# A third buffer for W1 and W2, products of zeros at the lowest rank, a wider port rule in the planner, and new ranks

## The chip, the core and the metric

The kernel runs on one core of one Trainium2 chip. The metric is the device time of one execution in microseconds (us); less is better. The engines are TensorE (PE in the profile, with its weight loads as PEld), VectorE (DVE), ScalarE (ACT), GpSimd (POOL) and SyncE (SP), which issues nearly all transfers.

## What is computed

x has the shape (4, 2048, 256) in float32. An attention block, here a long convolution with a gate, and a grouped linear block follow one another, each behind a layer norm and with the input added again:

```python
uv = silu(layernorm(x) @ uv_w)
u, v = split(uv, 2, axis=-1)
# _tno: convolution of v along the sequence with a kernel that a small network gives
a = concatenate([t_zero, t_pos, zeros, t_neg])           # t_* = _rpe(position) * GAMMA ** |position|
y = irfft(rfft(a, n=2 * n) * rfft(v, n=2 * n))[:, :n]
x = x + (u * y) @ o_w
# grouped block: 8 groups of 1024 tokens, no activation between its two products
h1 = einsum('gmh,goh->gmo', layernorm(x) in groups, W1) + b1
h2 = einsum('gmo,gho->gmh', h1, W2) + b2
x = x + h2
```

`_rpe` is a network on the position: three layers of layer norm, silu and a 32x32 product, and an output layer of the same kind.

## The kernel before

The program has two parts. First, Python functions record operations, one list for all engines (`Recorder`, line 69, with the recorders V, G, A, T and S for DVE, POOL, ACT, PE and SP). Then `issue_order` (line 287) sorts the whole list, and one loop issues it. So nearly all instructions have the line L1123 in the profile; they are told apart by the names of their tiles.

The stages, in the words that the profile uses for their tiles:

- `rpe_network` (line 621) computes the kernel of the convolution at 4096 positions. Each of its four layers makes two products ph, ACT writes their squares sq and a copy d, PE sums the squares into pvar (products with 4 columns), DVE makes a reciprocal root by three Newton steps on 128x32 tiles (nve, nh, ny, nt) and spreads it to ne, PE transposes ne into pr, DVE multiplies d by pr, and ACT makes z, from which the next layer's ph comes. All constants of the network are in one transfer, par; the first ph needs w0, which DVE makes from par. `rpe_transform` (line 705) makes the spectrum am from the result.
- `stage_a` (line 570) loads a quarter of a batch (xa), normalizes it (st_a, mv_a, ve_a, rs_a, nb_a, xn_a), transposes it (pt_a, xnt), makes v through the product pv, and POOL adds and subtracts halves of v into c.
- `prepare` splits c into residues of the polynomial ring for one batch b and half h (ra and others). `stage_b` (line 883) does for each of eight residues r a product pf with a matrix from `mats`, two multiplications with am on DVE (y, far), a product acc back, and then combinations on DVE; its `end` makes four tiles tk with which POOL multiplies the gate gt. `gate` (line 873) makes gt from the product pu.
- `stage_d` (line 1025) makes the product po of gt and o_w, adds it to x, normalizes, and multiplies with the folded weights wt (product pff) into the output.
- `stage_w` (line 811) folds the two weight matrices of a group g into one: the product pw over eight pieces of the inner dimension, loaded in four pairs of transfers w1 and w2 (256 KB each, offsets 0, 2, 4 and 6). ACT adds a bias to each w1 in place. pw lies in the pool ps_w, which has a single buffer; the products of zeros (`warm`) write to a tile of the same buffer, so that a pw comes only after the last of them. DVE makes wt from pw at the end.

```python
w1s = io.tile([P, oc, D], F32, tag="w1", bufs=WB, name=f"w1_{g}_{o}")
S.dma_start(w1s, w1[g].rearrange("(p a) h -> p a h", a=na)[:, o : o + oc, :])
```

The profile calls both tiles w, without group and offset. Each of the two tags has WB buffers; with 2, piece 4 of a group waits until the products of piece 0 have read their buffers.

What sets the order: each operation has a rank, 20 times its batch plus a value from the table `PLACE` (line 156). `place` (line 273) looks up the most exact key, so "w.6.l.1" (group 6, loading, second pair) goes ahead of "w.6"; keys with "first" and "last" hold for batches 0 and 3 alone. `issue_order` then steps through a modelled run: of all operations whose inputs and buffers are there, it takes the one that can start earliest, and of those that can start at the same time the one of lowest rank. Its durations come from `Operation.cost` (line 116). Three details of this model are touched:

- `port`: an operation of DVE with two inputs of at least 64 columns in SBUF, and any operation of POOL with inputs, occupy one shared port in the model, one after the other.
- `COLD`, `IDLE`: after an idle of more than IDLE ns, PE's operations cost twice as much for COLD ns.
- A tile takes a buffer of its tag in the order of the lowest ranks of its operations.

Twelve products of zeros (`WARM_UP`) are recorded with the ranks "warm.0" to "warm.11", the lowest numbers of all or nearly so: they stand at the head of PE's queue, ahead of the first ph.

Of the kernel before, what the change touches and what calls it, by code (L numbers as in the profile page):

```python
# [48 lines left out]
WB = 2  # L49
# [57 lines left out]
class Operation:  # L107
# [8 lines left out]
    def cost(self, method):  # L116
# [7 lines left out]
        if self.engine == "DVE":  # L124
            if method.startswith("bn"):
                return (327, 83) if method == "bn_stats" else (92, 74)
            n = max(n, columns(self.ins[0])) if method == "tensor_reduce" else n
            self.port = sum(columns(a) >= 64 for a in self.ins) >= 2 and not any(psum)
            return 68 + 1.04 * n, 80
# [12 lines left out]
class Pool:  # L142
# [14 lines left out]
    "a.0": 1.74, "a.0.n": -2, "a.0.t": 0.4, "a.0.v": 1,  # L157
    "a.1": -2.67, "a.1.t": -4, "a.1.v": -2,
    "a.2": 2.51, "a.2.n": -1,
    "a.3": 4.46, "a.3.n": 0, "a.3.t": 3,  # L160
    "a.0 first": -99, "a.0.n first": -158, "a.0.t first": -185, "a.0.v first": -150,
    "a.1 first": -98, "a.1.n first": -78, "a.1.t first": -98, "a.1.v first": -91, "a.1.x first": -125,
    "a.2.c first": -82, "a.2.n first": -74, "a.2.t first": -85, "a.2.v first": -64, "a.2.x first": -97,
    "a.3.c first": -96, "a.3.n first": -136, "a.3.t first": -138, "a.3.v first": -106, "a.3.x first": -77,
    "b.0": 12.16, "b.0.0": 6.26, "b.0.0.p": 9, "b.0.2": 4.1, "b.0.2.p": 8, "b.0.3.m": 22, "b.0.3.p": 9.4,
    "b.0.3.y": 10, "b.0.4.m": 37, "b.0.4.p": 11, "b.0.4.y": 10, "b.0.5.m": 13.79, "b.0.5.p": 12.3, "b.0.5.y": 37,
    "b.0.6": 12.58, "b.0.6.p": 12.2, "b.0.7": 14.11, "b.0.7.m": 5,
    "b.1": 20.27, "b.1.0.m": 10.46, "b.1.0.p": 20, "b.1.0.y": 11, "b.1.2.m": 15.97, "b.1.2.p": 14.4, "b.1.2.y": 36,
    "b.1.3": 19.01, "b.1.3.p": 17, "b.1.4": 18.94, "b.1.4.p": 15, "b.1.5.m": 16, "b.1.5.p": 18.98, "b.1.5.y": 18.2,
    "b.1.6": 22, "b.1.6.m": 37, "b.1.7": 20.97,  # L170
    "b.0 last": 12.58, "b.0.0.p last": 2, "b.0.1 last": 12.16, "b.0.1.y last": 17, "b.0.2.p last": 29,
    "b.0.3.m last": -4, "b.0.3.p last": 6, "b.0.3.y last": 13, "b.0.4 last": 8.37, "b.0.4.m last": 8.37,
    "b.0.4.p last": 8.37, "b.0.4.y last": 7, "b.0.5 last": 13.79, "b.0.5.p last": 13.79, "b.0.5.y last": 15,
    "b.0.6.p last": 12.58, "b.0.7.m last": 14.11, "b.0.7.p last": 9,
    "b.1 last": 75, "b.1.0.p last": 8, "b.1.1.p last": 30, "b.1.1.y last": 44, "b.1.2.p last": 25,
    "b.1.2.y last": 18.6, "b.1.3.p last": 36, "b.1.3.y last": 25, "b.1.4.p last": 42.8, "b.1.5 last": 18.98,
    "b.1.5.m last": 18.98, "b.1.5.p last": 18, "b.1.5.y last": 18.98, "b.1.6.m last": 33, "b.1.6.p last": 47,
    "b.1.6.y last": 44, "b.1.7.m last": 75, "b.1.7.p last": 59, "b.1.7.y last": 34,
    "d.0": 27.7, "d.0.n": 25.35, "d.0.o": 26.3, "d.0.t": 27.5, "d.0.x": 25.35,
    "d.1": 28.74, "d.1.f": 29.5, "d.1.n": 28, "d.1.o": 27, "d.1.x": 26.25,  # L180
    "d.2": 30.44, "d.2.f": 38.1, "d.2.o": 32, "d.2.s": 33.54, "d.2.t": 35.4,
    "d.3": 29.38, "d.3.f": 34, "d.3.o": 31.2, "d.3.s": 31.46, "d.3.t": 33,
    "d.0 last": 42.27, "d.0.f last": 64, "d.0.n last": 42.27, "d.0.o last": 65, "d.0.t last": 45,
    "d.0.x last": 42.27,
    "d.1 last": 140.66, "d.1.f last": 140.66, "d.1.n last": 135, "d.1.o last": 131, "d.1.x last": 65.21,
    "d.2.f last": 44, "d.2.n last": 90, "d.2.o last": 73, "d.2.t last": 88, "d.2.x last": 46.22,
    "d.3.f last": 57, "d.3.n last": 129, "d.3.o last": 74, "d.3.t last": 95, "d.3.x last": 61.26,
    "e.0.0": 22, "e.0.1": 18.21, "e.0.2": 18.05, "e.0.3": 16.77, "e.0.4": 27, "e.0.5": 86, "e.0.6": 77.59,
    "e.0.7": 13, "e.0.8": 12.6, "e.0.9": 18, "e.0.10": 17,
    "e.1": 22, "e.1.0": 45, "e.1.1": 20.5, "e.1.2": 20.8, "e.1.3": 31, "e.1.4": 21.4, "e.1.5": 47, "e.1.8": 24,  # L190
    "e.1.9": 30.7, "e.1.10": 26.75,
    "e.0.0 last": 30, "e.0.4 last": 63.85, "e.0.5 last": 71.2, "e.0.7 last": 28, "e.0.8 last": 23, "e.0.9 last": 29,
    "e.0.10 last": 13.2,
    "e.1.0 last": 46, "e.1.1 last": 100.83, "e.1.2 last": 31, "e.1.3 last": 65, "e.1.4 last": 105,
    "e.1.5 last": 111.26, "e.1.6 last": 74, "e.1.7 last": 34, "e.1.8 last": 43, "e.1.9 last": 57, "e.1.10 last": 72,
    "f.0": 2.08, "f.0.1.m": 36, "f.0.1.p": 4, "f.0.1.y": 2.91, "f.0.2": -2, "f.0.2.m": 1.13, "f.0.3.m": 2.05,
    "f.0.3.p": 0, "f.0.3.y": 2, "f.0.4.m": 35, "f.0.4.p": 8, "f.0.4.y": 4, "f.0.5.m": 7, "f.0.5.p": 5,
    "f.0.5.y": 3.57, "f.0.6.m": 58, "f.0.6.p": 9, "f.0.6.y": 8, "f.0.7.m": 6.26, "f.0.7.p": 7.8, "f.0.7.y": 11,
    "f.1": 8, "f.1.0.m": 49, "f.1.0.y": 4.04, "f.1.1.m": 18.16, "f.1.1.p": 16, "f.1.1.y": 15.3, "f.1.2.m": 13.91,
    "f.1.2.p": 12, "f.1.3": 13, "f.1.3.m": 14.02, "f.1.4": 14.8, "f.1.4.p": 15, "f.1.5.m": 14.19, "f.1.5.p": 14.9,  # L200
    "f.1.5.y": 12, "f.1.6": 17.79, "f.1.6.y": 16, "f.1.7.m": 18.04, "f.1.7.p": 17, "f.1.7.y": 15,
    "f.0 last": 0, "f.0.0.m last": 2.08, "f.0.0.p last": -1, "f.0.0.y last": -3.7, "f.0.1 last": 2.91,
    "f.0.1.m last": 2.91, "f.0.1.p last": 0, "f.0.2 last": 1.13, "f.0.2.y last": 0, "f.0.3 last": 2.05,
    "f.0.3.p last": 2.05, "f.0.3.y last": 0, "f.0.4 last": 4, "f.0.4.m last": 4, "f.0.4.p last": 4,
    "f.0.4.y last": 0, "f.0.5.m last": 23, "f.0.5.p last": 6.9, "f.0.5.y last": 10, "f.0.6.m last": 0,
    "f.0.6.p last": 36, "f.0.6.y last": 6.5, "f.0.7.m last": 27, "f.0.7.p last": 12, "f.0.7.y last": 8,
    "f.1 last": 18.16, "f.1.0.m last": 4.04, "f.1.0.p last": 45, "f.1.0.y last": 1, "f.1.1.p last": 15,
    "f.1.1.y last": 18.16, "f.1.2.p last": 17, "f.1.2.y last": 14.6, "f.1.3.p last": 12.04, "f.1.3.y last": 19,
    "f.1.4.m last": 22, "f.1.4.p last": 17.7, "f.1.5.m last": 28, "f.1.5.p last": 16, "f.1.5.y last": 14.19,
    "f.1.6.p last": 43, "f.1.6.y last": 28, "f.1.7.p last": 37, "f.1.7.y last": 22,  # L210
    "g.0.0": 6.5, "g.0.1": 12.71, "g.0.2": 15.72, "g.0.3": 7.2,
    "g.1.0": 17.8, "g.1.1": 10.75, "g.1.2": 19, "g.1.3": 22.6,
    "g.0 first": -66, "g.0.0 first": -66, "g.0.1 first": 7, "g.0.2 first": -66, "g.0.3 first": -70,
    "g.1.0 first": -95, "g.1.1 first": -86, "g.1.2 first": -55, "g.1.3 first": -107,
    "p.0.0": 55.79, "p.0.1": 1.74, "p.0.2": 54, "p.0.3": 23.91, "p.0.4": 1.63, "p.0.5": 19.64, "p.0.6": 38.78,
    "p.0.7": 19.76, "p.0.8": 4.06, "p.0.9": 16.19, "p.0.10": 6.7, "p.0.11": 33.43, "p.0.12": 39.59, "p.0.13": 31,
    "p.0.14": 7, "p.0.15": 33.61,
    "p.1.0": 7, "p.1.1": 7.6, "p.1.2": 14, "p.1.3": 67.54, "p.1.4": 11.67, "p.1.5": 13, "p.1.6": 14.31, "p.1.7": 15,
    "p.1.8": 15.07, "p.1.9": 18.9, "p.1.10": 70.61, "p.1.11": 20.64, "p.1.12": 27, "p.1.13": 20.4, "p.1.14": 35,
    "p.1.15": 19,  # L220
    "p.0.0 first": 21.76, "p.0.1 first": -38, "p.0.2 first": -23, "p.0.3 first": -3.8, "p.0.4 first": -3.5,
    "p.0.5 first": -50, "p.0.6 first": -84.19, "p.0.7 first": -44, "p.0.8 first": -2.3, "p.0.9 first": -34,
    "p.0.10 first": -15, "p.0.11 first": -13, "p.0.12 first": -1.1, "p.0.13 first": -0.8, "p.0.14 first": -0.5,
    "p.0.15 first": -7,
    "p.1 first": 4, "p.1.0 first": 14.03, "p.1.1 first": 4, "p.1.2 first": 3, "p.1.5 first": 6, "p.1.7 first": 4,
    "p.1.12 first": 18.53, "p.1.14 first": 45.22, "p.1.15 first": 80,
    "rpe": -100,
    "rpe.0": -190,
    "rpe.1": -153,
    "rpe.2": -145,  # L230
    "rpet": -74,
    "rpet.0": -3, "rpet.0.m": -5,
    "rpet.1": -25, "rpet.1.m": -10,
    "rpet.2": -53, "rpet.2.m": -10,
    "rpet.3": -18, "rpet.3.m": -10,
    "rpet.4": -10,
    "rpet.5": 3, "rpet.5.m": 52,
    "rpet.6": -21, "rpet.6.m": -10,
# [27 lines left out]
    "warm.8": -100.1,  # L266
    "warm.9": -100.1,
    "warm.10": -99.1,
    "warm.11": -99,
}  # L270


# [953 lines left out]
```

## Time and profile before

| | |
|---|---|
| median of 3 runs | 591.65 us (587.73, 592.72, 591.65) |
| the profiled execution's own time | 591.77 us |
| its span in the profile | 589.9 us (1.87 us lie around it) |
| mean granted clock of TensorE | 0.986 of full speed |
| TensorE idle, waiting for w (pw) | 6.2 us, 2 times, longest 3.4 |
| transfers from SP of w | 64 of 256 KB, median 4.6 us to landing |
| DVE's products y<-y,far, 128x256 | 128, mean 441 ns |
| POOL's c<-v | 64, mean 1086 ns |
| POOL's gt<-gt,tk | 32, mean 1462 ns |

How to read it: busy times are sums over an engine, and TensorE's matmuls are pipelined. A row of the timeline is a run of equal instructions: start, time, engine, line, operation, tiles, count, and in brackets the idle time before it with the instruction that ended it. A float32 product 128x256 is two instructions in the profile, so the twelve products of zeros are 24. The granted clock is what the throttle gave to TensorE, 1.00 at full speed.

### The profile page before, as it was taken

To read this page: it belongs to the slowest core of one execution; us is meant where nothing else is said; L and a number is where in the kernel's file an instruction comes from. 1 tells how busy PE (TensorE), PEld (TensorE's weight loads), DVE (VectorE), ACT (ScalarE), POOL (GpSimd) and SP (SyncE) were. 2 spreads that over 40 slices of the span, in tenths; PEclk is the share of its full clock that TensorE was granted. 3 is DMA by queue.
4 is the path that set the end of the run, shared out by engine and by line. 5 is a ranking of instruction groups with operands and counts; after the bars stand their busy time and mean duration, and the time that the engine had idled before them with its cause. 6 is when DMAs were issued, how large, how long until landed. Compare 5 with 4: busy or idle time off the path is not lost.

```text
span 589.9 us, 8356 instructions
## 1 busy us (share of the span) xinstructions
PE 569.5 (97%) x2676; PEld 463.5 (79%) x2676; DVE 506.8 (86%) x1117; ACT 312.0 (53%) x822; POOL 170.5 (29%) x184
## 2 busy tenths in 40 slices
PE   7999999999997999999999999999999999999897
PEld 5776667888885788888888878888788888777785
DVE  3476987999999999999877999989769999979972
ACT  2678873245321852889456617886657237211161
POOL 1133240003567321212654110354361012011420
PEclk8799999999999999999999999999999999999799
DMA  7742356855462445164441453536714554433103
GB/s 221 218 108 74 89 166 180 237 163 161 132 174 80 106 156 193 54 231 145 152 133 35 146 178 91 170 115 179 237 40 123 172 161 124 145 124 111 51 19 125
DMA packets 40051, 81.36 MB, mean 138 GB/s; under 512 B 5700, under 2 KB 7236, under 8 KB 40008
## 3 DMA queue, kind: packets, MB, share of 16 engines
q1 hardware_dynamic: 39272, 79.91, 44.8%
q10 hardware_dynamic: 736, 0.92, 0.5%
q8 instruction: 21, 0.34, 0.2%
q14 instruction: 22, 0.18, 0.1%
HBM read 72.43 MB, written 8.39 MB: 137 GB/s over the span
## 4 chain that ended last, share of the span: by engine, by line
PE 82%; DVE 8%; DMA 4%; ACT 3%; issue 1%; POOL 1%; SPq 0%; ACTq 0%; DVEq 0%
PE pf L1123 16%; PE acc L1123 16%; PE pff L1123 9%; PE pv L1123 8%; PE po L1123 8%; PE pw L1123 8%; PE pu L1123 7%; DMA w<-in_L_ffn_W_dram 3%; PE pt_d L1123 2%; PE pt_a L1123 2%; PE pvar L1123 1%; PE pa L1123 1%; PE ph L1123 1%; DMA par<-in_rpe_par_dram 1%; DVE y L1123 1%
## 5 line engine op out<-in xcount | busy, mean ns | idle before, releaser
L1123 PE MATMUL acc<-mats,y 128*128 128x256 f32 (+1 forms) x512 | 115.6, 367 | 0.0
L1123 PEld LDWEIGHTS acc<-mats,y 128*128 128x128 f32 x512 | 92.3, 190 | 14.9 <-issue 2.9
L1123 POOL TENSOR_TENSOR c<-v 128x256 f32<-128x256 f32 x64 | 67.7, 1086 | 76.0 <-ACT v L1123 76.0
L1123 POOL TENSOR_TENSOR gt<-gt,tk 128x512 f32<-128x512 f32 x32 | 46.5, 1462 | 103.0 <-DVE tk L1123 103.0
L1123 PE MATMUL pw<-w,w 128*128 128x256 f32 x256 | 69.0, 405 | 7.0 <-DMA w<-in_L_ffn_W_dram 6.2
L1123 PEld LDWEIGHTS pw<-w,w 128*128 128x128 f32 x256 | 49.9, 204 | 16.5 <-ACT w L1123 7.4
L1123 PE MATMUL pf<-ra,mats 128*128 128x256 f32 x256 | 61.2, 379 | 0.0
L1123 PE MATMUL pv<-uvw,xnt 128*128 128x256 f32 x256 | 60.8, 382 | 0.4 <-ACT xnt L1123 0.3
L1123 PE MATMUL po<-ow,gt 128*128 128x256 f32 x256 | 60.2, 380 | 1.0 <-POOL gt L1123 0.8
L1123 PE MATMUL pff<-wt,xn 128*128 128x256 f32 x256 | 60.1, 380 | 1.0 <-ACT xn L1123 1.0
L1123 PE MATMUL pu<-xnt,uvw 128*128 128x512 f32 x128 | 60.5, 595 | 0.3 <-ACT xnt L1123 0.3
L1123 ACT ACTIVATE w<-w,dw 128x256 f32<-128x256 f32 x64 | 29.6, 504 | 56.8 <-DMA w<-in_L_ffn_W_dram 56.6
L1123 PEld LDWEIGHTS po<-ow,gt 128*128 128x128 f32 x256 | 47.9, 190 | 10.1 <-POOL gt L1123 2.2
L1123 PEld LDWEIGHTS pv<-uvw,xnt 128*128 128x128 f32 x256 | 47.7, 190 | 9.6 <-ACT xnt L1123 1.5
L1123 PEld LDWEIGHTS pff<-wt,xn 128*128 128x128 f32 x256 | 48.1, 190 | 8.6 <-ACT xn L1123 1.8
L1123 PEld LDWEIGHTS pf<-ra,mats 128*128 128x128 f32 x256 | 48.1, 190 | 8.1 <-issue 1.3
L1123 DVE TENSOR_TENSOR y<-y,far 128x256 f32<-128x256 f32 x128 | 51.5, 441 | 0.1
L1123 POOL TENSOR_TENSOR rs_d<-ve_d,mhalf 128x4 f32<-128x4 f32 x16 | 17.7, 1109 | 105.6 <-ACT ve_d L1123 94.5
L1123 DVE TENSOR_TENSOR y<-pf,am 128x512 f32<-128x512 f32 x56 | 38.2, 683 | 7.2 <-PE pf L1123 3.8
L1123 POOL TENSOR_TENSOR rs_a<-ve_a,mhalf 128x4 f32<-128x4 f32 x16 | 22.9, 1433 | 70.4 <-ACT ve_a L1123 51.6
L1123 ACT ACTIVATE v<-pv 128x512 f32<-128x512 f32 x32 | 18.4, 591 | 43.0 <-PE pv L1123 19.6
L1123 DVE TENSOR_TENSOR far<-pf,am 128x512 f32<-128x512 f32 x56 | 38.1, 680 | 0.4 <-PE pf L1123 0.4
(153 smaller groups left out, 1021.5 us busy)
## 6 DMA issues: line engine op xcount, KB each, us to landing
mats<-in_mats_dram SPq DMA_DIRECT2D x128, 256.0 KB, 2.8
w<-in_L_ffn_W_dram SPq DMA_DIRECT2D x64, 256.0 KB, 4.6
xa<-in_x_dram SPq DMA_DIRECT2D x18, 512.0 KB, 4.2
xd<-in_x_dram SPq DMA_DIRECT2D x14, 512.0 KB, 3.8
out_dram<-xd SPq DMA_DIRECT2D x12, 512.0 KB, 3.1
mats_rpe<-in_mats_dram SPq DMA_DIRECT2D x8, 256.0 KB, 5.4
row<-in_L_ffn_b_dram SPq DMA_DIRECT2D x8, 128.0 KB, 4.5
ph<-in_phases_dram SPq DMA_DIRECT2D x8, 128.0 KB, 6.5
```

The costliest lines, as they stand in the source:

```text
L1123: ops[k].call(*ops[k].args, **ops[k].kw)
```

## The change

No operation of the computation is added, removed or altered; eight more products of zeros are made. Four things change.

1. `WB` is 3: the tiles w1 and w2 have three buffers each.
2. In the model, an operation of DVE with two inputs in SBUF takes the port from 4 columns on, not from 64.
3. Twenty products of zeros are recorded instead of twelve. The first has the rank -199, the others 1000: they have the last place among all that PE could start at a time, and are taken whenever the model sees PE with nothing else to start. `COLD` is 3500 instead of 5500.
4. The table `PLACE` has new values throughout. The lines that concern the network, the early stages, group 1, 2, 6 and 7 of `stage_w`, and the zeros:

```diff
-WB = 2
+WB = 3
...
-            self.port = sum(columns(a) >= 64 for a in self.ins) >= 2 and not any(psum)
+            self.port = sum(columns(a) >= 4 for a in self.ins) >= 2 and not any(psum)
...
-    "a.0 first": -99, "a.0.n first": -158, "a.0.t first": -185, "a.0.v first": -150,
+    "a.0 first": -99.0, "a.0.n first": -156.0, "a.0.t first": -143.0, "a.0.v first": -141.0,
...
-    "rpe": -100,
-    "rpe.0": -190,
-    "rpe.1": -153,
-    "rpe.2": -145,
+    "rpe": -100.0,
+    "rpe.0": -195.0,
+    "rpe.1": -153.0,
+    "rpe.2": -148.0,
+    "rpe.3": -143.0,
...
-    "w.1": -95.3, "w.1.l": -89, "w.1.l.0": -135, "w.1.l.1": -78, "w.1.l.2": -55, "w.1.l.3": -95, "w.1.m.1": -95.2,
-    "w.1.m.2": -85.7, "w.1.m.3": -95, "w.1.s": -94.9,
-    "w.2": 43.16, "w.2.l": -55, "w.2.l.0": 43.16, "w.2.l.1": 43.26, "w.2.l.2": 43.36, "w.2.l.3": 43.46,
-    "w.2.m.0": 26, "w.2.m.1": 33, "w.2.m.2": 28, "w.2.m.3": 34, "w.2.s": 43.56,
+    "w.1": -95.3, "w.1.l": -104.0, "w.1.l.0": -148.0, "w.1.l.1": -95.2, "w.1.l.2": -59.0, "w.1.l.3": -95.0,
+    "w.1.m.1": -107.0, "w.1.m.2": -87.0, "w.1.m.3": -95.0, "w.1.s": -94.9,
+    "w.2": 43.16, "w.2.l": -82.0, "w.2.l.0": 35.0, "w.2.l.1": 43.26, "w.2.l.2": 43.36, "w.2.l.3": 43.46,
+    "w.2.m.1": 24.0, "w.2.m.2": 27.0, "w.2.m.3": 43.46, "w.2.s": 75.0,
...
-    "w.6": 91.91, "w.6.l.1": 136, "w.6.l.2": 139, "w.6.l.3": 166, "w.6.m.0": 109, "w.6.m.1": 114, "w.6.m.2": 116,
-    "w.6.m.3": 118, "w.6.s": 95.91,
-    "w.7": 189.4, "w.7.l.0": 156, "w.7.l.1": 190.4, "w.7.l.2": 191.4, "w.7.l.3": 192.4, "w.7.m.1": 156,
+    "w.6": 91.91, "w.6.l.1": 92.91, "w.6.l.2": 93.91, "w.6.l.3": 94.91, "w.6.m.0": 97.0, "w.6.m.1": 92.91,
+    "w.6.m.2": 93.91, "w.6.m.3": 94.91, "w.6.s": 95.91,
+    "w.7": 189.4, "w.7.l.1": 190.4, "w.7.l.2": 191.4, "w.7.l.3": 192.4, "w.7.m.0": 142.0, "w.7.m.1": 147.0,
     "w.7.m.2": 191.4, "w.7.m.3": 192.4, "w.7.s": 193.4,
-    "warm.0": -199,
...
-    "warm.11": -99,
+    "warm": 1000.0,
+    "warm.0": -199.0,
...
-COLD, IDLE, WARM_UP = 5500, 1800, 12
+COLD, IDLE, WARM_UP = 3500, 1800, 20
```

## The prediction

> **What bounds the kernel now.** I read the page first: the busy shares, the row of granted clocks and the chain that ended last.
>
> ```profile
> PE 569.5 (97%) x2676; PEld 463.5 (79%) x2676; DVE 506.8 (86%) x1117; ACT 312.0 (53%) x822; POOL 170.5 (29%) x184
> ...
> PEclk8799999999999999999999999999999999999799
> ...
> PE 82%; DVE 8%; DMA 4%; ACT 3%; issue 1%; POOL 1%; SPq 0%; ACTq 0%; DVEq 0%
> ```
>
> TensorE works 97% of the span, and its clock is low in two places only, near the start and near the end. So time is to be had from TensorE's work, from its idle time and from its clock. The waits of PE come next:
>
> ```profile
> PE pw L1123 <- DMA w<-in_L_ffn_W_dram: 6.2, 2, 3.4
> PE pr L1123 <- DVE ne L1123: 2.3, 4, 0.7
> PE ph L1123 <- DVE w L1123: 2.2, 1, 2.2
> ```
>
> These are the waits that the change touches: twice a product pw waits for a load of W1 or W2 (6.2 us), and the first ph waits 2.2 us for par, while the products of zeros are over. What the waits cost is read in their own stages. The timeline of PE at the start, and two windows of the clock (columns: window, then busy time of PE, PEld, DVE, ACT, POOL, then the clock, DMA share, GB/s):
>
> ```profile
> 1.19 6.93 PE L1123 MATMUL warm<-zeros 128*128 128x256 f32 x24 [1.19 <-DVE zeros L1123]
> 10.30 3.08 PE L1123 MATMUL ph<-lag_t,w 4*128 4x512 f32 x4 [2.19 <-DVE w L1123]
> 13.30 3.57 PE L1123 MATMUL pvar<-par,sq 128*128 128x4 f32 x16
> 16.74 4.61 PE L1123 MATMUL pw<-w,w 128*128 128x256 f32 x10
> ```
>
> ```profile
> 9.00:10.00 1.00, 0.00 (x0) 0.00 (x0) 0.79 (x4) 0.00 (x0) 0.00 (x0) 1.00 0.78 257
> 11.00:12.00 1.00, 1.00 (x2) 0.34 (x2) 1.00 (x5) 0.29 (x1) 0.61 (x3) 0.52 0.91 105
> 21.00:22.00 1.00, 1.00 (x7) 0.83 (x6) 0.34 (x2) 0.15 (x1) 0.00 (x0) 0.86 0.48 148
> ```
>
> The zeros end at 8.12, PE idles 2.19 us, and from about 11.0 to 21.24 the granted clock is 0.50. Later a product 128x256 (two instructions) takes 0.427 us; here ten instructions of pw take 4.61 us, 0.85 to 0.92 a product. The stages of the two load waits, and the last one's rows:
>
> ```profile
> 10.00:20.00 10.00, 9.70 (x28) 6.88 (x29) 5.62 (x29) 5.82 (x12) 1.63 (x4) 0.55 0.96 252
> 180.00:190.00 10.00, 7.16 (x30) 5.26 (x29) 9.97 (x19) 1.41 (x3) 8.79 (x2) 1.00 0.23 54
> 540.00:550.00 10.00, 6.61 (x26) 5.42 (x25) 9.77 (x21) 3.31 (x7) 0.00 (x0) 0.85 0.43 121
> 550.00:560.00 10.00, 10.00 (x39) 8.44 (x39) 8.65 (x17) 0.00 (x0) 6.15 (x4) 0.81 0.00 0
> ```
>
> ```profile
> 547.85 6.17 PE L1123 MATMUL pw<-w,w 128*128 128x256 f32 x14 [3.39 <-DMA w<-in_L_ffn_W_dram]
> 553.86 2.32 PE L1123 MATMUL po<-ow,gt 128*128 128x256 f32 x10
> ```
>
> PE idles 2.84 us before 187.02, without loss of clock, and 3.39 us before 547.85, after which the clock is low for 6.8 us (546.9 to 553.7). In both windows DVE is busy 9.8 to 10 of 10 us: the load is not the only thing that PE is short of there.
>
> **The change, part by part.** The sum is made against the profiled execution, 591.77 us (span 589.9, 1.87 around it), which stands 0.12 above the median 591.65.
>
> *Products of zeros.* Twelve become twenty: 8 x 0.427 = 3.4 us more PE work. In the program's new order 18 lie ahead of the first ph, one between the halves of the first pvar and one behind it. Six more end at 8.12 + 6 x 0.427 = 10.7. SyncE now issues b and row of group 1 (0.33 + 0.43 us in its timeline) ahead of par, so I let par, which landed at 9.09, come about 0.9 later, and with it ph: 10.30 becomes 11.2, an idle of 0.5 us instead of 2.19. Bounds of this term: 0.4 (the zeros alone) and 1.7 (the two transfers also delay par's bytes). I take 0.9. The first loads of x move behind these too: xa of tile 0 from issue 3.21 to 7.1 or later. Its statistics are due only in the second layer, where DVE had 4.12 us of idle before the second Newton chain.
>
> *The clock.* With an idle of 0.5 us I expect it to hold. The first layer took 26.80 - 10.30 = 16.5 us, the next 12.4 (26.80 to 39.21): -4.1. Bounds: 0 (it falls anyway, a rival below) and -5.1, half of the 10.24 us at half speed. The Trainium skill, "TensorE: Matmul & The Clock Gate" (Part 1, "What's actually happening"), says that the clock gate looks at free-running windows of 3.4 us, drops after an idle one and rises after a busy one. The trace agrees in the distance of the changes but not in the rest: a gap of 2.19 us sufficed, and three windows from 11.0 on with PE busy throughout, on ph with 4 rows and pvar with 4 columns, did not raise it. By the rule as written a gap shorter than 3.4 us would have cost nothing, and this term would be 0.
>
> *Work inside the first layer.* ScalarE now does the two biases of W1 ahead of the first square: its stretch from the first ph to d grows from 4.71 to 5.52 us by the rows' durations, +0.8; DVE's batch-norm operations inside the first Newton chain grow from 0.12 to 1.08 us, +1.0. Each lies partly beside the other engine's part. Bounds: 0 and 1.8; I take 0.5, nearer the lower end, since 0.63 us of ACT's waiting for ph stands there before. The end of the position network is so 0.9 - 4.1 + 0.5 = **-2.7 us** earlier. PE's own tally gives the same or more (-5.1 of clock, +0.9, +0.85 for the two zeros inside the layer: -3.4). I keep the smaller.
>
> *Three buffers, group 2 (near 187).* Three pairs of loads now come early, and the wait of pieces 0 to 4 goes. But piece 6 takes the buffer of 4 or an earlier one that the order releases last, right ahead of piece 6 on PE, and the loads of group 4 stand ahead of it in SyncE's queue. From release to first use a load took 5.3 us in both waits of before (issue, transfer, bias on ACT): so an idle of about 5.4 instead of 2.84 + 0.35. Cover: the gates for the next po are ready 11.9 us after the last backward product of that half, and 8.5 us of PE work stand ahead of it, so 3.4 us are free. Cost 5.4 - 3.4 = 2.0, and with the small gap left before it (0.2) **+2.2**. Bounds: 0, the gates come later still; +7.3, no cover and half clock for 3.4 to 3.8 us behind (+1.9).
>
> *Port flag.* Only the planner's times change: operations of 4 to 63 columns now wait for the port in the model. No instruction is added on DVE (1119 issued by the program before and after), ACT, POOL or SP. What the flag is about is seen here: the last of these runs beside GpSimd's c.
>
> ```profile
> 32.70 0.19 DVE L1123 TENSOR_TENSOR nt<-ny 128x32 f32<-128x32 f32 x1
> 32.93 0.19 DVE L1123 TENSOR_TENSOR nt<-nt,nve 128x32 f32<-128x32 f32 x1
> 33.15 0.63 DVE L1123 SCALAR_TENSOR_TENSOR ny<-nt,ny 128x32 f32<-128x32 f32 x1
> ```
>
> ```profile
> 33.01 2.77 POOL L1123 TENSOR_TENSOR c<-v 128x256 f32<-128x256 f32 x4 [5.23 <-ACT v L1123]
> ```
>
> In the whole kernel such stretching adds 18.5 us to DVE, in 32 operations. The operations still meet; I count 0, with bounds -2 and +3.
>
> *Ranks, 200 to 530.* No load there has less than 4 us between its landing and PE's need, and PE's work is the same in number. DVE's work stands 0 to 1 us earlier than PE's in places and 2 to 3 us later near 400 to 500. I take **0** since what DVE delivers just in time stays so; the bounds are those just given.
>
> *The end.* Ten instruction pairs of pw of group 6 (4.3 us) now stand behind the last acc, where group 7 alone stood. Group 7's pieces have three buffers: piece 0 has 4.3 us of PE work ahead and waits 5.3 - 4.3 = 1.0; 2 and 4 come with it; 6 has 3.4 and waits 1.9. That is 2.9 us in two pieces against 3.39 + 3.4 (half of 6.8 at half clock) = 6.8 before, so -3.9; wt of group 6 (0.66 us) now lies in DVE's chain ahead of the last tk, of which I charge 0.5. Sum **-3.4**. Bounds: -1.5, the wait's true price before, since gt was ready at about 552.3 and po began at 553.86; -5, the waits are nothing.
>
> Sum: -2.7 + 2.2 + 0 - 3.4 = -3.9, and 591.77 - 3.9 = **587.9 us**.
>
> **The rivals.**
> - *Faster by more.* The gates near 187 cover the whole load (0 instead of +2.2), and the middle gains 1 to 2. For it: before, PE waited for gt there as well. Against: piece 6 has no work ahead. 591.77 - 2.7 - 3.4 - 1.5 = 584.2, or 581 with the whole 5.1 of clock.
> - *The clock falls anyway*, so that the zeros don't do what they are for. For it: ph and pvar did not raise it, perhaps they cannot hold it either. Then -4.1 goes: 592.0. Any account by which the gap of 2.19 us was not the cause gives the same. The Trainium skill's page named above is one such account.
> - *Load and clock near 187, slower.* The idle of 5.4 is uncovered and longer than the 3.39 that cost the clock at 547: 5.4 + up to 5.1 (the ten us at half speed of the start). It decides once the gates are ready more than 3 us ahead of PE. 591.77 - 2.7 + 10.5 - 3.4 = 596.2.
> - *DVE becomes the bound between 200 and 500, slower.* It is 96 to 100% busy for long stretches, and its results come 0.05 to 0.4 us ahead of PE's need. If the new order makes stretched operations half as many again (+9), or holds PE twice by 3.4 us with a loss of clock each (2 x 5), the sum is 597 to 602. It decides from 0.4 us of delay on.
>
> **How the numbers follow.** Forecast 0.33 (its own range 584 to 592), faster by more 0.17, clock falls 0.20, load and clock 0.13, DVE 0.17. One per cent, 585.7 and 597.6, is about what a measurement can tell here. Faster: 0.17 and a third of the forecast, 0.28. Slower: nearly all of DVE (0.16) and 0.04 of the load rival, 0.20. Within: 0.52. The range 580 to 599 leaves out the far ends of the first and the last rival, some 0.15.
>
> **What would show it.** Clock 1.00 from 8 to 25 and the second ph at 23 to 24.5 confirm the zeros; 0.50 there is the second rival. A wait pw from DMA of about 5.4 us near 180 to 190, and how low the clock is behind it, decides the third term. The last acc near 533 and two waits of 1 to 2 us behind it, with the clock at 1.00, confirm the end. The forecast is wrong if PE's waits for DVE between 200 and 530, under 3 us in all before, come to 5 us or more.

## The result, and the profile after

The changed kernel takes 587.38 us (median of 18 runs, 585.35 to 588.32) against 591.25 us (18 runs, 587.73 to 593.93): the ratio is 0.9926, with a 95% interval of 0.9911 to 0.9940, so 3.9 us or 0.7% less. The forecast was 587.9. The profiled execution took 585.86 us (span 584.1) and lies 1.5 us below its median; the profile of before lay on its own. So the two profiles differ by 5.9 us where the medians differ by 3.9, and no stage of these two pages should be read to better than 2 us. Why single executions differ so is told below.

The page's lines that answer to those of before:

```profile
PE 570.5 (98%) x2692; PEld 464.2 (79%) x2692; DVE 500.9 (86%) x1117; ACT 312.4 (53%) x822; POOL 160.2 (27%) x184
...
PEclk9899999999998899999999999999999999999999
...
PE 92%; DVE 3%; DMA 3%; ACT 1%; issue 1%; SPq 0%; ACTq 0%; DVEq 0%
```

TensorE works 1.0 us longer in a span that is 5.8 us shorter: its idle time fell from 20.4 to 13.6 us, though eight products of zeros (3.4 us) were added. DVE, with the same 1117 instructions, is busy 5.9 us less and GpSimd 10.3 us less. Single rows show operations of the two engines that take less time where they no longer run side by side: one c near 180 takes 8.15 us before the change and 0.87 after it, and rows of DVE stand further below. The clock is low in the slices near 20 and 185, no longer near 550. TensorE's waits:

```profile
PE pw L1113 <- DMA w<-in_L_ffn_W_dram: 4.6, 1, 4.6
PE warm L1113 <- DVE zeros L1113: 1.2, 1, 1.2
PE pw L1113 <- ACT w L1113: 1.0, 2, 0.7
PE ph L1113 <- ACT z L1113: 0.9, 1, 0.9
```

One wait for a load is left where there were two (6.2 us), and pr and the first ph wait no more. The start, in TensorE's timeline and in windows of 1 us:

```profile
1.19 10.08 PE L1113 MATMUL warm<-zeros 128*128 128x256 f32 x36 [1.19 <-DVE zeros L1113]
11.20 1.98 PE L1113 MATMUL ph<-lag_t,w 4*128 4x512 f32 x4
13.11 1.05 PE L1113 MATMUL pvar<-par,sq 128*128 128x4 f32 x8
14.02 0.68 PE L1113 MATMUL warm<-zeros 128*128 128x256 f32 x2
14.53 0.95 PE L1113 MATMUL pvar<-par,sq 128*128 128x4 f32 x8
15.34 0.97 PE L1113 MATMUL warm<-zeros 128*128 128x256 f32 x2
16.37 2.08 PE L1113 MATMUL pw<-w,w 128*128 128x256 f32 x4
```

```profile
9.00:10.00 1.00, 1.00 (x6) 0.90 (x5) 0.86 (x4) 0.64 (x2) 0.25 (x2) 1.00 0.98 312
11.00:12.00 1.00, 1.00 (x4) 0.48 (x3) 0.00 (x0) 0.00 (x0) 0.00 (x0) 1.00 0.90 318
14.00:15.00 1.00, 1.00 (x9) 0.95 (x9) 0.97 (x6) 0.87 (x2) 0.56 (x1) 1.00 1.02 344
17.00:18.00 1.00, 1.00 (x4) 0.82 (x3) 0.86 (x6) 0.89 (x2) 0.88 (x1) 0.50 1.05 241
```

The first ph starts at 11.20, where the forecast put it. The clock holds through the first layer's narrow products, then falls all the same, from 15.6 to 19.0. The two later stages (columns as before: PE, PEld, DVE, ACT, POOL, clock, DMA share, GB/s), and TensorE's timeline at the end:

```profile
10.00:20.00 10.00, 9.94 (x43) 6.83 (x42) 7.76 (x39) 5.17 (x11) 2.03 (x2) 0.83 1.00 284
180.00:190.00 10.00, 5.37 (x18) 3.59 (x17) 9.63 (x19) 2.72 (x6) 1.79 (x1) 0.81 0.58 147
540.00:550.00 10.00, 8.86 (x39) 6.94 (x38) 8.87 (x15) 2.72 (x6) 4.46 (x3) 1.00 0.45 119
550.00:560.00 10.00, 10.00 (x51) 8.18 (x51) 9.12 (x31) 3.34 (x7) 3.31 (x4) 1.00 0.01 2
```

```profile
533.67 4.48 PE L1113 MATMUL pw<-w,w 128*128 128x256 f32 x20
537.99 1.03 PE L1113 MATMUL po<-ow,gt 128*128 128x256 f32 x4
539.69 1.97 PE L1113 MATMUL pw<-w,w 128*128 128x256 f32 x8 [0.68 <-DVE wt L1113]
541.96 4.07 PE L1113 MATMUL pw<-w,w 128*128 128x256 f32 x16 [0.30 <-ACT w L1113]
546.73 1.97 PE L1113 MATMUL pw<-w,w 128*128 128x256 f32 x8 [0.70 <-ACT w L1113]
```

Behind the last acc TensorE has pw of group 6 and then group 7 to do, with short gaps at full clock. Before, the clock was 0.85 and 0.81 in the last two of these windows.

**Where the time came from.** An account that does not depend on what stands where: at any time, the time that has gone by less the work that TensorE has done, each product at its price at full clock (0.427 us for 128x256, others in proportion to their columns; 542.5 us in all). Products of few columns have next to no price, so most of their time counts as lost, in all kernels alike. What is left is lost, to idleness, to a low clock, or to products of zeros beyond the first twelve. The losses by stage, in us, up to TensorE's last product, from one profile of each kernel below; a cut is good to about 0.3 us. The first four have the order of the kernel before, the others the new one or nearly so:

| kernel | 0 to 170 | 170 to 200 | 200 to 530 | 530 to the end | median time, us |
|---|---|---|---|---|---|
| before | 23.4 | 4.7 | 7.2 | 8.4 | 591.25 |
| before, 18 zeros | 21.3 | 4.8 | 8.1 | 7.6 | 590.38 |
| before, 3 buffers in memory | 19.7 | 5.6 | 6.9 | 8.7 | 590.59 |
| before, less DVE work | 23.7 | 4.4 | 7.6 | 7.4 | 590.81 |
| after | 19.0 | 8.2 | 6.1 | 4.6 | 587.38 |
| after, 12 zeros | 20.7 | 8.4 | 6.3 | 4.5 | 587.28 |
| after, 18 zeros | 18.5 | 8.8 | 6.1 | 4.6 | 585.99 |
| after, 26 zeros | 24.0 | 8.4 | 6.3 | 4.8 | 588.36 |
| after, two loads moved | 20.9 | 7.9 | 6.8 | 4.5 | 587.83 |
| after, more DVE work | 20.4 | 7.8 | 11.3 | 4.6 | 592.83 |
| after, one rank changed | 20.4 | 8.9 | 8.5 | 4.2 | 590.37 |
| after, old port flag | 21.1 | 8.3 | 8.3 | 4.3 | 590.89 |

The last stage is the same in all eight profiles of the new order (4.2 to 4.8) and in all four of the old one (7.4 to 8.7): there the change gains 8.0 - 4.5 = 3.5 us on the means. The middle gives about 1 where the new order is kept as it is. The first 200 us give nothing, because two changes pull against each other there. Up to 170 the new order loses less, 20.6 against 22.0 on the means, with a scatter of 4 us and more within each order. From 170 to 200 it loses more in every profile, 7.8 to 8.9 against 4.4 to 5.6, which is 3.4 us on the means.

### The profile page after: what moved, and what is told of

It is laid out like the page before. It is cut to its first block, busy times and chain, and to the rows that moved or that the text cites. A ratio compares the mean times of both kernels' runs of the same rounds, so it can differ in the third digit from the quotient of the medians.

```text
span 584.1 us, 8353 instructions
## 1 busy us (share of the span) xinstructions
PE 570.5 (98%) x2692; PEld 464.2 (79%) x2692; DVE 500.9 (86%) x1117; ACT 312.4 (53%) x822; POOL 160.2 (27%) x184
## 4 chain that ended last, share of the span: by engine, by line
PE 92%; DVE 3%; DMA 3%; ACT 1%; issue 1%; SPq 0%; ACTq 0%; DVEq 0%
PE pf L1113 18%; PE acc L1113 17%; PE pff L1113 10%; PE pv L1113 9%; PE pw L1113 8%; PE pu L1113 8%; PE po L1113 8%; DMA w<-in_L_ffn_W_dram 3%; PE pt_d L1113 2%; PE pt_a L1113 2%; PE warm L1113 2%; PE pa L1113 2%; PE hp L1113 1%; PE ph L1113 1%; PE pvar L1113 1%; DVE yc L1113 1%
## 5 line engine op out<-in xcount | busy, mean ns | idle before, releaser
L1113 POOL TENSOR_TENSOR c<-v 128x256 f32<-128x256 f32 x64 | 55.4, 891 | 84.3 <-ACT v L1113 81.2
L1113 PE MATMUL pw<-w,w 128*128 128x256 f32 x256 | 66.0, 394 | 6.5 <-DMA w<-in_L_ffn_W_dram 4.6
L1113 PEld LDWEIGHTS pw<-w,w 128*128 128x128 f32 x256 | 48.4, 198 | 18.7 <-ACT w L1113 8.3
L1113 POOL TENSOR_TENSOR rs_d<-ve_d,mhalf 128x4 f32<-128x4 f32 x16 | 22.2, 1388 | 129.1 <-ACT ve_d L1113 112.0
L1113 ACT ACTIVATE gt<-pu 128x512 f32<-128x512 f32 x32 | 19.0, 592 | 50.7 <-PE pu L1113 50.7
L1113 DVE TENSOR_TENSOR y<-pf,am 128x512 f32<-128x512 f32 x56 | 38.5, 687 | 4.3 <-PE pf L1113 3.6
L1113 POOL TENSOR_TENSOR rs_a<-ve_a,mhalf 128x4 f32<-128x4 f32 x16 | 18.9, 1180 | 84.3 <-ACT ve_a L1113 73.4
```

What stands on the lines that cost most here:

```text
L1113: ops[k].call(*ops[k].args, **ops[k].kw)
```

## The experiments

In the kernels that begin with a_ (from the changed kernel) and b_ (from the one before) the planned order is held: it is computed as in that kernel, and the edit is made when the instructions are issued. In those that begin with e_ the planner orders anew.

**a_zeros12.** The changed order with only the first twelve products of zeros.

```diff
+    zs = [k for k, o in enumerate(ops) if o.outs[0].tensor.name.startswith("warm")]
     with tc.manual_schedule():
-        for k in issue_order(ops, tags):
+        for k in [k for k in issue_order(ops, tags) if k not in zs[12:]]:
```

> The changed kernel with its order of instructions held, but only the first twelve products of zeros made. Theory 1 (the zeros are worth their clock): TensorE idles 2 to 3 us ahead of the first ph, which still starts near 11.1, the granted clock is 0.50 from about 11 to 20, the first layer takes 16.3 us instead of 13.7, and the time is 2.5 us longer, 589.9. Rival (the order of the ranks brings the gain, and the eight zeros are 3.4 us of work that nothing needs): no change or a little less, 586.5 to 587.4.

Measured: 587.28 us, ratio to before 0.9941 (0.9919 to 0.9963). In its profile the start is what theory 1 said:

```profile
10.80 3.35 PE L1113 MATMUL ph<-lag_t,w 4*128 4x512 f32 x4 [2.58 <-DVE w L1113]
14.08 3.57 PE L1113 MATMUL pvar<-par,sq 128*128 128x4 f32 x16
17.52 2.05 PE L1113 MATMUL pw<-w,w 128*128 128x256 f32 x4
```

TensorE idles 2.58 us, the clock is 0.50 from 11.3 to 21.5, the second ph starts at 26.61 and the network's end (pz) at 60.27 instead of 58.58. The time is the changed kernel's by the medians and 0.9 us more by the ratios, whose intervals allow -0.7 to +2.4 us. So the 2.5 us of theory 1 are just outside, but a gain of 1 to 2 us by the zeros isn't ruled out, and the rival isn't shown either.

**a_zeros18.** The same with `zs[18:]`: the two zeros inside the first layer are left out.

> The changed kernel with its order held, without the two products of zeros inside the first layer. Theory 1: they fill time in which TensorE would wait for ScalarE, but they do not hold the clock, which falls at about 15.8 with or without them: 587.0 to 587.4. Rival (they are what keeps the clock up between 12 and 15.8): the clock falls at 12.4, one stretch of 3.4 us earlier, and the time is 1.3 to 1.7 us longer, 588.9.

Measured: 585.99 us, ratio 0.9922 (0.9901 to 0.9944); the clock is low from 16.3 to 19.7, a stretch as long as with them. The time is below both ranges, but by the ratios it is the changed kernel's (0.2 us less). The two zeros inside the layer do nothing that can be measured, as theory 1 had it.

**b_zeros18.** The order before, with the twelfth product of zeros made seven times: eighteen ahead of the first ph.

> The kernel before with its order held, and six more products of zeros at the head of TensorE's queue: eighteen, as the changed kernel has ahead of its first ph. Theory 1: the first ph starts at 10.75 instead of 10.30, the clock stays at 1.00 to about 15, the first layer takes 13.7 us instead of 16.5, and the time is 2.3 us shorter, 589.0. Rival (the gain needs the new order): the layer is as long as before and the time 591.3 to 592.

Measured: 590.38 us, ratio 0.9992 (0.9974 to 1.0010). The second ph starts at 24.64 instead of 26.80 and pz at 60.73 instead of 62.88, as theory 1 said; the time does not follow. The six zeros change it by -1.5 to +0.6 us, not by the -2.3 that were expected. The clocks of all runs say why, by an estimate: the mean is 0.992 here and 0.988 in the runs of the kernel before beside them (before rounding, 0.0034 apart), which is 2.0 us of 588 and not the 3.4 between the two profiles, and the first ph starts 1.1 us later (11.42 against 10.30). That leaves some 0.9 us, within the interval.

**b_buf3.** The order before, planned with two buffers, but with three in memory.

```diff
-        t = self.pool.tile(shape, dtype, name=name, **kw)
+        t = self.pool.tile(shape, dtype, name=name, **{**kw, **({"bufs": 3} if kw.get("tag") in ("w1", "w2") else {})})
```

> The kernel before with its order held, planned with two buffers, but with three buffers for W1 and W2 in memory. Both waits of pw for a load should be gone. Theory 1: the wait near 187 was covered by the gates and brings nothing, the one near 547 brings the 1.5 to 3.4 us that the forecast gave to the end: 588 to 589.8. Rival A (both were covered): 591. Rival B (both cost their full length and the clock behind the second): 581.6.

Measured: 590.59 us, ratio 0.9990 (0.9971 to 1.0010): rival A. The timeline of its end shows why:

```profile
537.77 5.34 PE L1123 MATMUL pw<-w,w 128*128 128x256 f32 x24
544.56 1.53 PE L1123 MATMUL pw<-w,w 128*128 128x256 f32 x6 [1.45 <-DMA w<-in_L_ffn_W_dram]
549.24 4.07 PE L1123 MATMUL po<-ow,gt 128*128 128x256 f32 x10 [3.14 <-POOL gt L1123]
```

The wait for the load shrinks from 3.39 to 1.45, and po waits 3.14 for the gates instead. Near 187 the wait for the load is gone, and po waits 3.42 us for gt there. So both waits of the kernel before were covered, the one near 187 wholly: there po came 0.06 us after the first gate. At the end it came 1.6 us after it (552.26 and 553.86); in b_buf3 it comes at once, but the clock is low behind it (549.9 to 553.3). Removing the waits alone changes the time by -1.7 to +0.6 us.

This profile shows something else. Its first 10 us have the same instructions as the kernel before, with twelve zeros, and yet they differ: the 24 instructions of zeros take 8.37 us instead of 6.93, the first ph waits 0.69 instead of 2.19, the clock is low from 14.0 to 17.4 instead of 11.0 to 21.3, and the second ph stands 3.3 us earlier.

```profile
1.18 8.37 PE L1123 MATMUL warm<-zeros 128*128 128x256 f32 x24 [1.18 <-DVE zeros L1123]
10.24 1.98 PE L1123 MATMUL ph<-lag_t,w 4*128 4x512 f32 x4 [0.69 <-DVE w L1123]
23.46 1.99 PE L1123 MATMUL ph<-z,bd 128*128 128x512 f32 x4 [1.07 <-ACT z L1123]
```

So the second ph comes earlier here without one zero more than with six more (24.64) or with all eight (24.91). What a profile shows of the zeros' gain in the first layer depends on which execution it caught. Over all profiles the zeros do help: of the five kernels with twelve zeros four (the kernel before among them) are low for 10.24 us at the start, and this one for 3.41; the eight with 18 or 20 zeros are all low for 3.41.

**e_piece6.** One rank changed, `"w.2.m.3": 43.46` to `38.5`, so that the last load of group 2 goes ahead of group 4's.

> The changed kernel with one rank changed, so that the last pair of loads of group 2 stands ahead of the loads of group 4 and its buffer comes from an earlier piece; the planner orders anew from there. Theory 1: the wait of 4.6 us near 188 and the low clock behind it go, which is 3.0 us by the tally of lost time, 584.4. Rival (the gates were as late as the load): the wait becomes one for gt and the time stays at 587.

Measured: 590.37 us, ratio 0.9993 (0.9974 to 1.0012), 4.0 us worse than the changed kernel by the ratios. The wait for the load is gone and this one stands in its place:

```profile
PE po L1113 <- POOL gt L1113: 5.4, 1, 5.4
```

So the gates were nearly as late as the load. That the time also grew was foreseen by neither theory: with one rank changed, some hundred rows of TensorE's order differ, and the table shows the loss in the middle (8.5 instead of 6.1) and in the first 200 us (29.3 instead of 27.2).

**a_zeros26.** The changed order with each of the two inner zeros made four times.

> The changed kernel with its order held, each of the two products of zeros inside the first layer made four times: six more, 2.6 us of work. This asks what the clock gate counts. Theory 1 (the clock falls at 15.8 because TensorE had too little dense work in the 3.4 us before): it stays at 1.00 through 16 to 19, which gives 1.7 us back, against up to 2.6 us of zeros in the way: 587.5 to 588.5. Rival (it is the narrow products, ph with 4 rows and pvar with 4 columns, that bring it down whatever lies between them): 0.50 there as before, and 589 to 590.

Measured: 588.36 us, ratio 0.9961 (0.9937 to 0.9985), within theory 1's range. In ten of its twelve runs the mean granted clock was 0.997, against 0.987 to 0.994 in the changed kernel's; the profile caught one of the other two, with 0.987 and a time of 591.52 us, so its row in the table is not typical. There the clock is low from 14.8 to 21.6, earlier and for longer than with two zeros, so how the other ten kept it up, and where, isn't shown. On the mean the clock was won and the time was not: by the ratios the kernel is 2.1 us longer, with 2.6 us of zeros more.

**e_port64.** `>= 4` back to `>= 64` in the port flag, all else as changed.

> The changed kernel with the port flag as before (from 64 columns on); ranks, zeros and buffers new; the planner orders anew. If the flag is what keeps GpSimd's c out of the Newton chains of layers 3 and 4, those layers take 2 to 3.2 us longer again and the time is 589.5 to 590.5. If the ranks alone do that, the layers stay at 10.4 and 10.0 us and the time within 1 us of 587.4.

Measured: 590.89 us, ratio 0.9998 (0.9981 to 1.0014). The third layer takes 12.2 us from ph to ph, as before the change (12.5), not 10.4; DVE's busy time is back near before:

```profile
PE 570.6 (97%) x2692; PEld 463.1 (79%) x2692; DVE 505.3 (86%) x1117; ACT 312.9 (53%) x822; POOL 160.7 (27%) x184
```

The fourth layer stays short, 10.3 us. Without the flag the new ranks gain nothing in time. But e_piece6 lost as much by one rank, with DVE at 502.4, so this run does not show that the 4.4 us of DVE time are what costs the 4 us.

**e_b_port.** The new flag with everything else as before.

> The kernel before with the new port flag alone; the planner orders anew with the old ranks. If the flag is what matters, the Newton chains of layers 3 and 4 are no longer stretched and the time is 588 to 589. Rival (ranks are fitted to one model, and another model with the old ranks disturbs the rest of the order): the chains are shorter, and the time is the same or longer, 591 to 595.

Measured: 598.54 us, ratio 1.0120 (1.0090 to 1.0149): worse than the rival's range. The third and fourth layer take 10.6 and 10.2 us, so the chains are shorter, as both theories had it; with e_port64 this shows that the flag is what shortens the third layer, with the old ranks and with the new. DVE as a whole is busy 509.5 us, more than before. The ranks, fitted to the model without the flag, order worse with it: the last stage loses 12.2 us. Behind the last acc TensorE has only 24 instructions of products (5.1 us), and then this wait:

```profile
PE po L1123 <- POOL gt L1123: 5.0, 1, 5.0
```

After these eight a second theory was formed: DVE, busy 97 to 100% for long stretches, sets the pace, and the 5.9 us less of it are the gain.

**a_far7.** The changed order, the eight products far of batch 1, half 0 made twice.

```diff
-            ops[k].call(*ops[k].args, **ops[k].kw)
+            for _ in range(2 if ops[k].outs[0].tensor.name.startswith("far_1_0_") else 1):
+                ops[k].call(*ops[k].args, **ops[k].kw)
```

> The changed kernel with its order held; DVE makes the eight products far of batch 1, half 0, twice each, with the same result: 8 x 0.60 = 4.8 us more DVE work between 205 and 260, where DVE is busy 97 to 100%. Theory 2 (formed after the first eight runs: in the long middle DVE sets the pace and TensorE only follows, so that less stretching of DVE's operations is what the change gives): 3.5 to 4.8 us longer, 591 to 592. Rival (TensorE, busy 98%, sets the pace, DVE has room): up to 1 us, 587.4 to 588.4.

Measured: 592.83 us, ratio 1.0011 (0.9991 to 1.0032): 5.0 us more than the changed kernel by the ratios, for 4.8 us of DVE work. In the changed kernel DVE has no slack there.

**a_c2.** The same edit for GpSimd's 64 operations c.

> The changed kernel with its order held; GpSimd makes each of its 64 operations c twice, with the same result: 64 x 0.7 = 45 us more at the shared port, and each c ready 0.7 us later. DVE's operations lie 9.9 us of their durations longer beside c in the changed kernel. Theory 2: the stretch beside c about doubles, DVE's busy time grows by 7 to 10 us and the time by 4 to 9 us, 591 to 596. Rival (what is stretched has slack): DVE's busy time grows as much, and the time by at most 1 us, 587.4 to 588.4.

Measured: 615.03 us, ratio 1.0391 (1.0358 to 1.0424): 27.5 us more. The page:

```profile
PE 580.5 (95%) x2692; PEld 468.1 (76%) x2692; DVE 520.2 (85%) x1117; ACT 313.0 (51%) x822; POOL 217.4 (35%) x248
```

DVE's 1117 instructions take 19.3 us longer, twice what was expected, and new waits of TensorE for DVE's xd and ne and for ScalarE's v appear. A longer GpSimd queue costs through the port and through later results; the run does not part the two.

**a_load6.** The changed order, but the last pair of loads of group 2 and its bias moved ahead of group 4's loads.

> The changed kernel with its order held but for the last pair of loads of group 2 and its bias on ScalarE, which go ahead of group 4's. This prices the wait of 4.6 us near 188 with nothing else moved. Theory 2 (DVE and GpSimd finish the gates no earlier than the load comes): the wait goes to po, for gt, with the same end, 586.5 to 588. Rival (the third term of the forecast): 2 to 3 us shorter, 584.4 to 585.4.

Measured: 587.83 us, ratio 0.9922 (0.9892 to 0.9952). No gain, but it isn't the clean price that was wanted: the bias now stands so early in ScalarE's queue that ScalarE waits 8.15 us for the load, v comes late, and TensorE waits as long at po:

```profile
PE po L1117 <- ACT v L1117: 4.1, 1, 4.1
```

**b_noy.** The order before, without the sixteen operations y<-y,far of batch 1, half 0 (that part of the spectrum's product is left out).

> The kernel before with its order held, without the sixteen operations y<-y,far of batch 1, half 0 (so y lacks far there): 8 x 0.72 = 5.8 us less DVE work between 205 and 265, and nothing else changed. Theory 2 (DVE sets the pace before the change as well, so that taking 4.8 us of stretch off DVE can be worth the 3.9 us of the change): 4 to 5.8 us shorter, 585.5 to 587.5. Rival (TensorE sets the pace in the kernel before): at most 1 us, 590.2 to 591.4.

Measured: 590.81 us, ratio 1.0018 (0.9996 to 1.0041): the rival, and theory 2 falls too. Two windows, of the kernel before and then of this one:

```profile
210.00:220.00 10.00, 10.00 (x56) 8.97 (x55) 10.00 (x19) 4.50 (x10) 3.58 (x3) 1.00 0.47 154
220.00:230.00 10.00, 10.00 (x47) 8.07 (x46) 9.97 (x20) 0.58 (x1) 2.33 (x1) 1.00 0.47 174
```

```profile
210.00:220.00 10.00, 10.00 (x55) 8.95 (x55) 8.80 (x16) 4.49 (x10) 3.40 (x3) 1.00 0.47 157
220.00:230.00 10.00, 10.00 (x46) 8.11 (x45) 9.60 (x18) 0.59 (x1) 1.39 (x1) 1.00 0.45 172
```

DVE has room now (8.80 and 9.60), and TensorE is at 10.00 of 10 with and without. In the middle both engines are full: work added on DVE cost its length (in the changed kernel), and work taken off it gave nothing (in the kernel before), where TensorE had no idle time to lose. What follows is argued and not shown: less stretching of DVE can pay only where TensorE waits for a chain of DVE and GpSimd, in the position network, at the gates near 190, and at the end.

## Why the prediction was right, and where its working was not

The number, the direction and the largest term hold. As losses of TensorE by stage, the four parts of the sum came out at -1.4 up to 170 (forecast -2.7), +3.4 near 187 (+2.2), -1.1 in the middle (0) and -3.5 at the end (-3.4), from one profile of each kernel. But the reasons given for the first two did not hold, and that the sum met the time to half a microsecond is in part luck. The terms, one by one:

- *Products of zeros and the clock, -2.7.* The first ph came at 11.20, as forecast, but not by the way forecast: there is no idle of 0.5 us, since the 36 instructions of zeros ran up to it (10.08 us). Without the later zeros ph could start at 10.80 (a_zeros12), so par came 0.5 us later and not 0.9; that the number fits is luck. The clock held to 15.6 and not to 25. The second ph came 1.9 us earlier than before, at 24.91, and the network's end 4.3 us earlier, at 58.58. The other 2.4 us are the later layers, which no term had: the second grew from 12.41 to 13.20, the third and fourth fell from 12.47 to 10.42 and from 11.20 to 10.05. The step that failed is the -4.1 for the clock. It let the clock hold, where a stretch of 3.41 us at half speed stayed, and it priced the 10.24 us of one profile as what the kernel always does; in b_buf3 the same first instructions run at half speed for 3.41 us, and the second ph comes at 23.46 with no zero more. On the mean clocks, the eight zeros are worth 1.4 us of half speed (0.9867 in a_zeros12, 0.9892 after), less the 0.4 by which ph starts later; measured are 0.9 us, within -0.7 to +2.4.
- *Three buffers near 187, +2.2.* The idle came, 4.63 us (forecast 5.4), with the clock low from 186.3 to 193.1. The step that failed is the cover. The forecast let the gates be ready 11.9 us after the last backward product; from the last acc (its end at 176.82) to the end of the first gate (190.79) it took 13.97. TensorE has 8.54 us of products for that time, as forecast, so it would have stood idle 5.4 us without any load. The load and the low clock behind it cost what po came later than that gate, 1.1 us; with the load in time (e_piece6) po came at once. First before, then after:

```profile
187.02 3.69 PE L1123 MATMUL pw<-w,w 128*128 128x256 f32 x16 [2.84 <-DMA w<-in_L_ffn_W_dram]
191.06 1.13 PE L1123 MATMUL po<-ow,gt 128*128 128x256 f32 x4 [0.35 <-POOL gt L1123]
```

```profile
188.35 3.75 PE L1113 MATMUL pw<-w,w 128*128 128x256 f32 x8 [4.63 <-DMA w<-in_L_ffn_W_dram]
191.89 1.41 PE L1113 MATMUL po<-ow,gt 128*128 128x256 f32 x3
```

  That the stage still lost 3.4 us more than before has another cause in the main: before, 10.25 us of products stood between that acc and po, after only 8.54, while the gates took as long (13.72 and 13.97). The new order took 1.7 us of work away from behind this acc, and the loss grew by that, by the 1.1 us, and by the low clock behind po.
- *Port flag, 0 within -2 and +3.* The stretch fell by more than was thought, DVE's busy time by 5.9 us. Flag and ranks did that together: DVE is busy 506.8 us before, 509.5 with the flag alone, 505.3 with all but the flag and 500.9 after. In the third layer the last Newton steps and ne are back at their plain lengths. First before, then after:

```profile
46.43 0.65 DVE L1123 TENSOR_TENSOR nt<-nt,nve 128x32 f32<-128x32 f32 x1
47.12 1.15 DVE L1123 SCALAR_TENSOR_TENSOR ne<-nt,ny 128x512 f32<-128x512 f32 x1
```

```profile
44.84 0.19 DVE L1113 TENSOR_TENSOR nt<-nt,nve 128x32 f32<-128x32 f32 x1
45.06 1.29 DVE L1113 SCALAR_TENSOR_TENSOR ne<-nt,ny 128x512 f32<-128x512 f32 x2
```

  The second row of before is one operation of 1.15 us, that of after is two in 1.29. The Trainium skill, "SBUF — State Buffer" (section "Who interferes with whom"), says that a DVE instruction with two SBUF inputs contends with a GpSimd instruction that reads SBUF, over a port pair that the two engines share. The traces agree: nt takes 0.65 us beside c and 0.19 without it. What the flag is worth in time by itself stays open; ranks and model belong together (e_port64, e_b_port).
- *The middle, 0.* It gave about 1 us (7.5 to 6.3 on the means of the kernels that keep the new order there). TensorE has no wait for DVE between 200 and 530 in the changed kernel, so the forecast's sign of being wrong did not come.
- *The end, -3.4.* Measured -3.5 on the means of eight and four profiles, but for a different reason than the forecast priced. It compared load waits (2.9 against 6.8 us), and b_buf3 shows that load waits had next to no price there; after the change TensorE waits 1.7 us in that stretch, in three pieces, and not 2.9 in two. What ends last there is the chain from the last acc through DVE's combinations and GpSimd's gates to po: 13.7 us before (540.15 to 553.86), 12.2 in b_buf3 (537.07 to 549.24), 14.7 after (533.83 to 548.53). In b_buf3 TensorE has 34 instructions of products to fill it with (34 x 0.2135 = 7.3 us), after the change 56 (12.0 us), mostly because ten products of pw of group 6 now stand behind the last acc (4.3 us, the number the forecast gave), and so the acc comes earlier by as much. e_b_port is a third point on this line: 24 instructions (5.1 us) behind the last acc, 13.6 us from it to po, and the greatest loss in the last stage, 12.2. So the chain takes 12 to 15 us in each of the three orders, and the loss falls as the products behind the acc grow, 5.1, 7.3 and 12.0 us; near 187 the same relation works against the change. That the moved products alone do this is argued from these rows; a kernel with only them moved wasn't tried.

Of the rivals, "the load is covered" was true as a mechanism but for 1.1 us, and did not bring its time, since it held before as well and the gates held TensorE longer. "The clock falls anyway" was half true, for 3.4 us. That DVE might become the bound in the middle was true in its price (a_far7: 5.0 us for 4.8) and did not come to pass.

## What to carry to other kernels

A wait in the profile is worth only what the next chain leaves of it: give the wait its cure with everything else held before pricing it, as b_buf3 did, and look for what the waiting engine would meet next. A stretch of low clock in one profile is not yet a price either: compare the mean clocks of several runs first. When the engine that waits has work that fits anywhere, put it behind the last product that starts the other engines' closing chain. When an order is planned from a model, ranks and model are one thing: parts of the change, each tried alone, gave nothing or lost up to 1.2%.

## What the runs showed of the hardware

The clock differs from execution to execution of one program. The mean granted clocks of all runs gather near 0.997, 0.994, 0.991, 0.988 and 0.985, steps of 0.003, which is what one stretch of 3.4 us at half speed takes from a span of 587 us (1.7 / 587). Of the 87 runs of the kernel before with a known clock, the 25 at 0.990 or more have a median of 589.5 us, the 43 at 0.987 to 0.988 one of 590.8, and the 19 below that one of 592.8: 1.3 to 2.1 us from group to group. That is a part of the spread of the times and not all of it: the 41 runs at 0.988 alone go from 587.8 to 593.1. A stretch of low clock in one profile is one draw of several, though not all draws are as likely (four of five profiles with twelve zeros are low for 10.24 us at the start); the forecast took it for a property of the program.

The clock also falls while TensorE is busy. In the changed kernel TensorE is busy for all of 11 to 15, on ph with 4 rows, pvar with 4 columns and a few zeros, and the clock falls at 15.6. The Trainium skill, "TensorE: Matmul & The Clock Gate" (Part 1, "What's actually happening"), gives the throttled state to an idle window of 3.4 us. The trace agrees with the length (3.4 us low), but no window here was idle, so idleness alone doesn't decide it; nor does a gap of 2.19 us, since in b_buf3 the clock fell behind one of 0.69. That it is how dense the products are is a guess: six more zeros between them go with a mean clock of 0.997 in ten of twelve runs, but in the one profiled the clock fell earlier (a_zeros26), and without any zeros between them it fell no sooner (a_zeros18). What the gate counts stays open.
